# Setup work before a first attention: where an image load, the scan constants and the weight tables stand in a four-layer kernel

## The chip, the cores and the metric

The kernel runs on one core of a Trainium2 chip. The metric is the device time of one execution in microseconds (us). Everything is single precision (f32).

## What is computed

A batch of four images of 128 channels and 64 x 64 pixels (4096 positions) goes through four residual layers. Each layer first group-normalises its input (32 groups of 4 channels).

```python
x = x + attention(gn(x), Wq, bq, Wk, bk, Wv, bv)      # 4096 x 4096 scores per image
x = x + conv5x5(gn(x), kernel_from(weightsxx, weightsidentity, XhatXhat, identity, inds...))
x = x + mamba(gn(x))     # Wx, 4-tap conv, silu, softplus, scan over 4096 steps; forward and reverse half
x = x + conv3x3(gn(x), main_w) + main_b
```

The 5x5 kernel is not given. It is built from two small radial tables: for each of 25 taps the table entry of the tap's radius, times a direction table, plus an identity part. The scan layer keeps 64 states for each of 2 x 64 channels: `h[t] = exp(delta[t]*A) * h[t-1] + delta[t]*x[t]*B[t]`, and `y[t] = sum over states of h[t]*C[t] + D*x[t]`.

## The kernel before

**Setup (L97 to L209).** The ScalarE queue loads the small inputs: `vec`, `wv`, `wm` (the transposed Wq, Wk, Wv, Wx), `wback`, `m3` (the 3x3 weights), `ssm`, `every` (the rates Alog, spread over partitions) and `bv`. From these the kernel makes `wqk` and `bqk` (needed by attention), and the constants of the scan layer: `a_neg`, `sel`, `skip` (L137 to L164), and `wtap`, `edge`, `cbias`, `hbias` (L190 to L209). `wtap` is Wx times each of the four convolution taps; each takes a small matmul (`ptap`, L195) and a VectorE multiply (L198). The pool `early`, which holds `wm`, is closed at L207, and only then are the pools `big` (whole images) and `bg` opened (L1040), so the image tile `x` lies on memory that `early` had.

**Stages.** `images()` (L1025) is one long Python generator of "work": for image 0 the attention, the 5x5 convolution and the preparation of the scan's operands, then the same for images 1, 2 and 3, then the ends and the 3x3 convolutions of images 0 to 2. Each step yields an estimated TensorE cost in us (PRODUCT 0.86 for a full matmul, SLOT 0.7, HOP 1.7). `scan_core` (L751) is the other generator: the scan of all four images as 1024 ticks, 256 an image. A tick is one product `db` on GpSimd (L808, 128 x 1024), two exponentials on ScalarE (L801), two scans on VectorE (L818), a product with C on VectorE (L821) or GpSimd (L839), and on every second tick four matmuls `y` on TensorE (L853). The main loop (L1088) takes half a tick and then as much work as a credit allows: PACE 2.9 cost units a tick, 1.5 for the last image. Instructions are put out in the order in which these generators are asked; each engine executes its own queue in that order.

**Attention of image 0 (L361)** runs before any scan. For each of 8 blocks of 512 queries it goes through 32 units; unit u does `scores(u)` (matmul L405, then exp to `pt` on ScalarE, L411), and `values(u-2)` (matmul L417). `pt` lies in a ring of 8 slots (NRING). In this first attention the softmax sums are collected by `side_sums` (L451): even units on VectorE (`sided`), odd units on GpSimd (`sidep`). The exponential of unit u+8 writes the slot of unit u, so it has to wait for the side sum of unit u. `queries` (L372) of the next block comes at unit 17 of each block.

**The 5x5 weights** are built by `build_conv_weights` (L214), a generator with 13 steps: 5 + 6 table rows (a tiny compare L238, a product L242/L244 and a sum L245 of 128 x 1600 each on VectorE), two steps for the identity and direction tables (L254, L255), and a last sum (L257). In `program` (L1062) one step of it is taken for every one unit of the attention, from the first unit on.

**Operands of the scan (L610).** For each image, eight pieces of 512 positions run through a hand-written plan of slots: piece i starts at slot 5i; its last step is at slot 5i + 13. The logarithms that finish softplus need another activation table than the exponentials, so they are batched: `logs` (L707) handles four pieces at a time (HM = 4), at slots 30 and 50. After `logs` come `join` and the store of delta, `drives` (GpSimd, L690) and the store of delta*x. The scan reads its operands back from DRAM, spread over partitions, in chunks c of 1024 positions (two pieces). It is let in by `before(b)` (L1073), once the first four pieces are through, at slot 35. A scan of 256 ticks goes through chunk 0 in its first 64 ticks, and so on.

Of the kernel before, what the change touches and what calls it, by code (L numbers as in the profile page):

```python
# [32 lines left out]
P = 128  # L33
GROUPS = 32
GN_EPS = 1e-5
CH = 1024
MM = 512
# [8 lines left out]
PRODUCT, HOP, SLOT, PACE, ENDPACE, AHEAD = 0.86, 1.7, 0.7, 2.9, 1.5, 4  # L46
# [6 lines left out]
def conv_preact_kernel(  # L53
# [16 lines left out]
    nc = tc.nc  # L70
# [4 lines left out]
    KC = 4  # L75
# [17 lines left out]
    def bank(tag, name):  # L93
        return pools.get(tag, ps).tile([P, MM], F32, tag=tag, name=name)
# [3 lines left out]
    nc.scalar.dma_start(vec, vecs)  # L98
    wv = const.tile([P, C], F32, name="wv")
    nc.scalar.dma_start(wv, mats[:, 2, :])  # L100
    setup = ExitStack()
    early = setup.enter_context(tc.tile_pool(name="early", bufs=1))
    wm = early.tile([P, 4, C], F32, name="wm")
# [21 lines left out]
    def col(i):  # L125
        return vec[:, i : i + 1]
# [10 lines left out]

    NK, NQ = P // SG, NST // NI
    a_neg = const.tile([P, NK * NQ], F32, name="a_neg")
    with tc.tile_pool(name="rates", bufs=1) as tmp:  # L140
        every = tmp.tile([P, NK, NQ, NI], F32, name="every")
        for k in range(NK):
            rates = vecs[k * SG : (k + 1) * SG, ALOG : ALOG + NST].unsqueeze(1)
            nc.scalar.dma_start(
                every[:, k].rearrange("p q j -> p (q j)"),
                rates.to_broadcast([SG, NI, NST]),
            )
        mine = tmp.tile([P, NI], F32, name="mine")
        nc.vector.tensor_reduce(
            mine, ident.rearrange("p (s i) -> p i s", i=NI), AX.X, ALU.add  # L150
        )
        every = every.rearrange("p k q i -> p (k q) i")
        mine = mine.unsqueeze(1).to_broadcast([P, NK * NQ, NI])
# [6 lines left out]
    nc.vector.tensor_reduce(  # L160
        sel, ident.rearrange("p (s i) -> p s i", i=NI), AX.X, ALU.add
    )
    skip = const.tile([P, P], F32, name="skip")
    nc.vector.tensor_scalar(skip, ident, col(DSKIP), None, ALU.mult)  # L164


    wqk = const.tile([P, C], F32, name="wqk")
# [22 lines left out]
    wtap = const.tile([P, KC, C], F32, name="wtap")  # L190
    edge = const.tile([P, KC - 1], F32, name="edge")
    cbias = small.tile([P, 1], F32, tag="cbias", bufs=1, name="cbias")
    for k in range(KC):
        ptap = bank("saz"[k % 3], f"ptap{k}")[:, :C]
        nc.tensor.matmul(  # L195
            ptap, col(CONVW + k).to_broadcast([P, P]), ident, start=True, stop=True
        )
        nc.vector.tensor_tensor(wtap[:, k, :], wm[:, 3, :], ptap, ALU.mult)  # L198
    for t in range(KC - 1):

        nc.vector.tensor_reduce(
            edge[:, t : t + 1], vec[:, CONVW : CONVW + KC - 1 - t], AX.X, ALU.add
        )
    nc.vector.tensor_tensor(cbias, edge[:, 0:1], col(CONVW + KC - 1), ALU.add)
    nc.vector.scalar_tensor_tensor(cbias, cbias, col(BX), col(CONVB), ALU.mult, ALU.add)
    nc.vector.tensor_scalar(edge, edge, col(BX), -1.0, ALU.mult, ALU.mult)
    setup.close()  # L207
    hbias = const.tile([P, 1], F32, name="hbias")
    nc.vector.tensor_scalar(hbias, cbias, 0.5, None, ALU.mult)  # L209


    cw = const.tile([P, NTAP, C], F32, name="cw")
# [397 lines left out]
    def scan_operands(b, xn, mats4, piece):  # L610
# [1 line left out]

        bc, dd, dxd, xcd, xsd = mats4
        pad = KC - 1
        HM = NM // 2

        xc = large(b, f"xc_{b}")[:, :L]
        delta = pools["big"].tile([P, L], F32, tag="xt", name=f"delta_{b}")
# [94 lines left out]
        def at(slot, f, *args):  # L713
            slots.setdefault(slot, []).append((f, args))

        EVERY = 5
        for i in range(NM):
# [22 lines left out]
        at(2, ready.add, (b, "read"))  # L740
# [10 lines left out]
    def scan_core(mats4, ynds, before, widen, result):  # L751
# [18 lines left out]
        def load(i):  # L770
            b, c, d, q, g = ticks[i]
            (bmat, cmat), dd, dxd, xcd, _ = mats4[b]
            if q == 0:
                for name, src in (("de", dd), ("dx", dxd)):
                    t = pools["rep"].tile([P, CH], F32, tag=name, name=f"{name}_{b}_{c}_{d}_{g}")
                    k = d * KG + g
                    src = src[c, k * SG : (k + 1) * SG].unsqueeze(1)
                    nc.sync.dma_start(t, src.to_broadcast([SG, NI, CH]))
                    rep[name, b, c, d, g] = t
            if g == 0:  # L780
                for name, src in (("b", bmat), ("c", cmat)):
                    t = pools["rows"].tile([P, CH], F32, tag=name, name=f"{name}r_{b}_{c}_{d}_{q}")
                    n = d * NST + q * NI
                    nc.sync.dma_start(t, src[c, n : n + NI].unsqueeze(0).to_broadcast([SG, NI, CH]))
                    rows[name, b, c, d, q] = t
            if d == 0 and q == NQ - 2 and g == 0:
                xcs[b, c] = pools["rows"].tile([P, CH], F32, tag="xc", bufs=1, name=f"xcr_{b}_{c}")
                nc.sync.dma_start(xcs[b, c], xcd[c])
# [134 lines left out]
    def program(safe):  # L923
# [113 lines left out]
            ready.add((B - 1, "staged"))  # L1037

        with ExitStack() as es, tc.manual_schedule():
            pools["big"] = es.enter_context(tc.tile_pool(name=f"big{safe}", bufs=1))  # L1040
            pools["bg"] = es.enter_context(tc.tile_pool(name=f"bg{safe}", bufs=2))
# [28 lines left out]
            pools["hc"] = es.enter_context(tc.tile_pool(name=f"hc{safe}", bufs=6))  # L1070
# [2 lines left out]
            def before(b):  # L1073

                nonlocal pace
                while (b, NM // 2) not in ready:
                    next(work)
                if b + 1 == B:
                    pace = ENDPACE
# [21 lines left out]
                pass  # L1101

    program(False)


    fit = small.tile([P, B * NJT], F32, tag="fit", bufs=1, name="fit")
# [71 lines left out]
```

## Time and profile before

| | |
|---|---|
| Time, median of 3 runs | 4684.2 us (4680.76 to 4685.26) |
| Span of the profiled run | 4679.2 us |
| First attention matmul of image 0 (L405) | 40.8 us |
| 5x5 convolution of image 0 (L571) | 542.4 to about 717.5 us |
| First scan instruction (L818) | 789.2 us |
| First attention matmul of image 1 | 812.1 us |
| Last `y` of the scan ends, then the end and 3x3 convolution of image 3 | 4597.6 us, until 4672.6 us |

The profile gives the busy time of each engine (PE is TensorE, PEld its weight loads, DVE VectorE, ACT ScalarE, POOL GpSimd, SP the queue of the synchronous engine), the span cut in 40 slices, groups of instructions by source line, waits with what ended them, and instructions in order of time. In a row of the timeline the first number is the start, the second the duration in us; what stands in square brackets at the end is the idle time before it, and what ended it.

### The profile page before, as it was taken

The page shows a single profiled execution, that of the slowest core. Times are in us where ns is not written, and L with a number is a line of the kernel's source. Part 1 is how long each engine was busy: PE and PEld are TensorE (multiplying, and loading weights), DVE is VectorE, ACT ScalarE, POOL GpSimd, SP SyncE. Part 2 cuts the span into 40 slices and gives each one's busy share as a digit, 9 for nine tenths or more (in the row PEclk, how much of TensorE's full clock was granted, in tenths as well). Part 3 has the DMA queues.
Part 4 walks back from the last instruction along what each step waited for, and adds up shares of the span by engine and source line. Part 5 has one row for each costly group of instructions (what it writes and reads, how often), then busy time and mean ns, then how long its engine had stood idle before and what let it go on. Part 6 is the DMA issues. An engine that isn't in the chain of part 4 may idle for free. (4 is left out here: it accounts for less than half of the span.)

```text
span 4679.2 us, 43928 instructions
## 1 busy us (share of the span) xinstructions
PE 4151.4 (89%) x13840; PEld 1538.3 (33%) x13840; DVE 3764.6 (80%) x3673; ACT 2313.3 (49%) x4166; POOL 3522.0 (75%) x1644
## 2 busy tenths in 40 slices
PE   6999997999999988999999979999999748576767
PEld 3444443333333323333333323333333202121212
DVE  7222104999999998999999999899989899999993
ACT  2333205666665356666654466666543644444431
POOL 2333202898888978898989869888889689999992
PEclk9999998999999999999999989999999968787878
DMA  1000005544444555445444564454445565656561
GB/s 65 0 0 1 0 5 184 186 168 163 163 169 150 178 203 214 155 164 175 169 158 164 187 227 169 157 177 164 168 147 177 201 224 199 229 193 229 186 230 46
DMA packets 210434, 718.90 MB, mean 154 GB/s; under 512 B 24848, under 2 KB 25744, under 8 KB 210064
## 3 DMA queue, kind: packets, MB, share of 16 engines
q1 hardware_dynamic: 208448, 714.69, 43.7%
q8 instruction: 111, 1.82, 0.2%
q10 hardware_dynamic: 1744, 1.32, 0.1%
q14 instruction: 131, 1.07, 0.1%
HBM read 649.07 MB, written 66.85 MB: 153 GB/s over the span
## 5 line engine op out<-in xcount | busy, mean ns | idle before, releaser
L808 POOL TENSOR_TENSOR db<-dx,br 128x1024 f32<-128x1024 f32 x1024 | 2404.4, 2367 | 377.8 <-DVE hc L818 94.8
L801 ACT ACTIVATE da<-de,a_neg 128x512 f32<-128x512 f32 (+1 forms) x1795 | 1343.9, 752 | 926.9 <-DVE da L818 600.3
L405 PE MATMUL sc<-r,x 128*128 128x512 f32 x2048 | 1087.5, 613 | 44.0 <-ACT last L834 16.4
L417 PE MATMUL acc<-pt,v 128*128 128x512 f32 x2048 | 1049.1, 594 | 1.5
L839 POOL TENSOR_TENSOR hc<-hc,cr 128x1024 f32<-128x1024 f32 x392 | 928.5, 2369 | 19.0 <-ACT last L834 15.5
L411 ACT ACTIVATE pt<-sc 128x512 f32<-128x512 f32 x1024 | 604.0, 590 | 613.4 <-PE sc L405 577.8
L821 DVE TENSOR_TENSOR hc<-da,cr 128x512 f32<-128x512 f32 (+1 forms) x1095 | 847.1, 774 | 71.7 <-DVE da L818 0.9
L853 PE MATMUL y<-hc,sel 128*32 128x512 f32 x4096 | 654.0, 653 | 272.7 <-POOL hc L839 247.5
L818 DVE TENSOR_TENSOR_SCAN da<-da,last,db 128x512 f32<-128x512 f32 (+1 forms) x474 | 740.5, 1562 | 16.2 <-POOL db L808 8.9
L571 PE MATMUL pce<-xpe,cw 128*128 128x512 f32 x1600 | 724.6, 606 | 24.8 <-ACT xpe L311 17.8
L818 DVE TENSOR_TENSOR_SCAN da<-da,da,db 128x512 f32<-128x512 f32 x463 | 595.8, 1287 | 26.2 <-ACT da L801 25.8
L405 PEld LDWEIGHTS sc<-r,x 128*128 128x128 f32 x2048 | 358.9, 190 | 642.7 <-issue 385.9
L417 PEld LDWEIGHTS acc<-pt,v 128*128 128x128 f32 x2048 | 388.4, 190 | 498.9 <-issue 480.0
L571 PEld LDWEIGHTS pce<-xpe,cw 128*128 128x128 f32 x1600 | 297.3, 190 | 452.4 <-issue 424.0
L818 DVE TENSOR_TENSOR_SCAN hc<-da,last,db 128x512 f32<-128x512 f32 (+1 forms) x294 | 442.7, 1506 | 2.9 <-POOL db L808 1.2
L818 DVE TENSOR_TENSOR_SCAN hc<-da,hc,db 128x512 f32<-128x512 f32 x308 | 395.1, 1283 | 45.1 <-ACT da L801 15.6
L459 POOL TENSOR_TENSOR sidep<-sidep,pt 128x512 f32<-128x512 f32 x120 | 161.3, 1344 | 307.0 <-ACT pt L411 307.0
L853 PEld LDWEIGHTS y<-hc,sel 128*32 128x32 f32 x4096 | 93.5, 111 | 728.7 <-POOL hc L839 333.2
L571 PE MATMUL pcm<-xpm,m 128*128 128x512 f32 x576 | 287.5, 647 | 31.4 <-ACT xpm L311 31.4
L459 DVE TENSOR_TENSOR sided<-sided,pt 128x512 f32<-128x512 f32 x120 | 90.3, 753 | 249.7 <-ACT pt L411 248.4
L818 DVE TENSOR_TENSOR_SCAN da<-da,db 128x512 f32<-128x512 f32 (+1 forms) x158 | 235.7, 1492 | 17.0 <-ACT da L801 9.3
L834 ACT COPY last<-da 128x1 f32<-128x1 f32 x473 | 74.0, 156 | 270.1 <-DVE hc L821 268.2
(167 smaller groups left out, 2251.9 us busy)
## 6 DMA issues: line engine op xcount, KB each, us to landing
br<-bm SPq DMA_DIRECT2D x512, 512.0 KB, 5.0
cr<-cm SPq DMA_DIRECT2D x512, 512.0 KB, 3.9
de<-dd SPq DMA_DIRECT2D x64, 512.0 KB, 4.6
dx<-dxd SPq DMA_DIRECT2D x64, 512.0 KB, 6.2
x<-in_x_dram SPq DMA_DIRECT2D x16, 512.0 KB, 5.7
xs<-in_x_dram SPq DMA_DIRECT2D x16, 512.0 KB, 6.8
xsd<-xs SPq DMA_DIRECT2D x16, 512.0 KB, 5.1
xcd<-xc SPq DMA_DIRECT2D x16, 512.0 KB, 2.7
```

The lines of the kernel that those rows point to most:

```text
L405: nc.tensor.matmul(sc, xn[:, bass.ts(j, P)], rq[blk], start=True, stop=True)
L411: nc.scalar.activation(pt, sc, AF.Exp)
L417: nc.tensor.matmul(acc[blk], v[:, j, :], ring[:, u % NRING, :], start=j == 0, stop=j == NJT - 1)
L459: eng.tensor_tensor(s, s, ring[:, u % NRING, :], ALU.add)
L571: nc.tensor.matmul(acc.rearrange("p (r w) -> p r w", w=W), weights[:, t, :], xp[:, y : y + RPM, dx : dx + W], start=t == 0, stop=t == k * ...
L801: nc.scalar.activation(da, rep["de", b, c, d, g][:, bass.ts(h, size)], AF.Exp, scale=a_neg[:, at(i)])
L808: nc.gpsimd.tensor_tensor(dbs[i], rep["dx", b, c, d, g], rows["b", b, c, d, q], ALU.mult)
L818: nc.vector.tensor_tensor_scan(h, da, db[:, cut], before, ALU.mult, ALU.add)
L821: nc.vector.tensor_tensor(hc[:, cut], h, rows["c", b, c, d, q][:, cut], ALU.mult)
L834: nc.scalar.copy(last[b][:, at(i)], end)
L839: nc.gpsimd.tensor_tensor(hcs[i], hcs[i], rows["c", b, c, d, q], ALU.mult)
L853: nc.tensor.matmul(y[r : r + SG, :], sel, hcs[i - KG + 1 + gg][:, bass.ts(h, MM)], start=q == 0, stop=False, tile_position=(0, r), skip_gr ...
```

## The change

Three parts. First, the pools `big` and `bg` are opened ahead of `early`, so that the tiles of the first image have memory of their own and their loads depend on nothing in the setup. Second, the constants of the scan leave the setup: they become a generator `scan_constants` of 8 steps, and the loop that ran `build_conv_weights` now runs both, one after the other, taking a step for every four units of the attention in place of one. Third, the operands of image 0's scan are let through in three groups, pieces 0-1, 2-5 and 6-7, and the scan enters when chunk 0 (a quarter) is there. For the other images the groups stay four and four.

```diff
+    lower = ExitStack()
+    pools["big"] = lower.enter_context(tc.tile_pool(name="big", bufs=1))
+    pools["bg"] = lower.enter_context(tc.tile_pool(name="bg", bufs=2))
     setup = ExitStack()
     early = setup.enter_context(tc.tile_pool(name="early", bufs=1))
...
-    with tc.tile_pool(name="rates", bufs=1) as tmp:
-        every = tmp.tile([P, NK, NQ, NI], F32, name="every")
...
-        nc.vector.tensor_tensor(every, every, mine, ALU.mult)
-        nc.vector.tensor_reduce(a_neg, every, AX.X, ALU.add)
-    nc.scalar.activation(a_neg, a_neg, AF.Exp)
-    nc.vector.tensor_scalar(a_neg, a_neg, -1.0, None, ALU.mult)
...
-    for k in range(KC):
-        ptap = bank("saz"[k % 3], f"ptap{k}")[:, :C]
...
-    setup.close()
...
+    def scan_constants():
+        for k in range(KC):
+            ptap = bank("z", f"ptap{k}")[:, :C]
+            nc.tensor.matmul(
+                ptap, col(CONVW + k).to_broadcast([P, P]), ident, start=True, stop=True
+            )
+            yield HOP
+            nc.vector.tensor_tensor(wtap[:, k, :], wm[:, 3, :], ptap, ALU.mult)
+        for t in range(KC - 1):
+            nc.vector.tensor_reduce(
+                edge[:, t : t + 1], vec[:, CONVW : CONVW + KC - 1 - t], AX.X, ALU.add
+            )
...
+        yield HOP
+        mine = early.tile([P, NI], F32, name="mine")
...
+        nc.vector.tensor_tensor(rates, rates, mine, ALU.mult)
+        nc.vector.tensor_reduce(a_neg, rates, AX.X, ALU.add)
+        yield HOP
+        nc.scalar.activation(a_neg, a_neg, AF.Exp)
...
+        nc.vector.tensor_scalar(skip, ident, col(DSKIP), None, ALU.mult)
+        yield HOP
+        nc.vector.tensor_scalar(a_neg, a_neg, -1.0, None, ALU.mult)
+        yield HOP
...
-        def logs(i):
-            for n in range(i, i + HM):
+        def logs(i, j):
+            for n in range(i, j):
                 nc.scalar.activation(us[n], us[n], AF.Ln)
...
-        for i in (0, HM):
-            t = EVERY * (i + HM - 1) + 15
-            at(t, logs, i)
-            for n, c in enumerate(range(i * MM // CH, (i + HM) * MM // CH)):
+        PER = CH // MM
+        cuts = (0, PER, NM - PER, NM) if b == 0 else (0, NM // 2, NM)
+        for i, j in zip(cuts, cuts[1:]):
+            t = EVERY * (j - 1) + 15
+            at(t, logs, i, j)
+            for n, c in enumerate(range(i // PER, j // PER)):
                 at(t + 1 + n, join, c)
                 at(t + 3 + n, drives, c)
-            at(t + 3 + HM * MM // CH, ready.add, (b, i + HM))
+                at(t + 4 + n, ready.add, (b, "operands", c))
...
                     with tc.tile_pool(name="tables", bufs=1) as tmp:
-                        for _ in build_conv_weights(tmp):
-                            next(work)
+                        for _ in chain(scan_constants(), build_conv_weights(tmp)):
+                            for _ in range(4):
+                                next(work)
                     while (0, "attended") not in ready:
                         next(work)
                 del pools["fill"]
+                setup.close()
...
             def before(b):
                 nonlocal pace
-                while (b, NM // 2) not in ready:
+                while (b, "operands", 0) not in ready:
                     next(work)
```

More of the change, by code (lines that the diff above doesn't have):

```diff
@@ L139, in conv_preact_kernel @@
     a_neg = const.tile([P, NK * NQ], F32, name="a_neg")
-    with tc.tile_pool(name="rates", bufs=1) as tmp:
-        every = tmp.tile([P, NK, NQ, NI], F32, name="every")
[L142 to L150, printed above, removed]
-        )
-        every = every.rearrange("p k q i -> p (k q) i")
-        mine = mine.unsqueeze(1).to_broadcast([P, NK * NQ, NI])
-        nc.vector.tensor_tensor(every, every, mine, ALU.mult)
-        nc.vector.tensor_reduce(a_neg, every, AX.X, ALU.add)
-    nc.scalar.activation(a_neg, a_neg, AF.Exp)
-    nc.vector.tensor_scalar(a_neg, a_neg, -1.0, None, ALU.mult)
+    every = early.tile([P, NK, NQ, NI], F32, name="every")
+    for k in range(NK):
+        rates = vecs[k * SG : (k + 1) * SG, ALOG : ALOG + NST].unsqueeze(1)
+        nc.scalar.dma_start(
+            every[:, k].rearrange("p q j -> p (q j)"),
+            rates.to_broadcast([SG, NI, NST]),
+        )
     sel = const.tile([P, SG], F32, name="sel")
-    nc.vector.tensor_reduce(
-        sel, ident.rearrange("p (s i) -> p s i", i=NI), AX.X, ALU.add
-    )
     skip = const.tile([P, P], F32, name="skip")
-    nc.vector.tensor_scalar(skip, ident, col(DSKIP), None, ALU.mult)
     wqk = const.tile([P, C], F32, name="wqk")
@@ L192, in conv_preact_kernel @@
     cbias = small.tile([P, 1], F32, tag="cbias", bufs=1, name="cbias")
-    for k in range(KC):
-        ptap = bank("saz"[k % 3], f"ptap{k}")[:, :C]
-        nc.tensor.matmul(
-            ptap, col(CONVW + k).to_broadcast([P, P]), ident, start=True, stop=True
-        )
-        nc.vector.tensor_tensor(wtap[:, k, :], wm[:, 3, :], ptap, ALU.mult)
-    for t in range(KC - 1):
+    hbias = const.tile([P, 1], F32, name="hbias")
+    def scan_constants():
[10 more added lines that the diff above has]
+            )
+        nc.vector.tensor_tensor(cbias, edge[:, 0:1], col(CONVW + KC - 1), ALU.add)
+        nc.vector.scalar_tensor_tensor(cbias, cbias, col(BX), col(CONVB), ALU.mult, ALU.add)
+        nc.vector.tensor_scalar(edge, edge, col(BX), -1.0, ALU.mult, ALU.mult)
+        nc.vector.tensor_scalar(hbias, cbias, 0.5, None, ALU.mult)
+        yield HOP
+        mine = early.tile([P, NI], F32, name="mine")
+        nc.vector.tensor_reduce(
+            mine, ident.rearrange("p (s i) -> p i s", i=NI), AX.X, ALU.add
+        )
+        rates = every.rearrange("p k q i -> p (k q) i")
+        mine = mine.unsqueeze(1).to_broadcast([P, NK * NQ, NI])
+        nc.vector.tensor_tensor(rates, rates, mine, ALU.mult)
+        nc.vector.tensor_reduce(a_neg, rates, AX.X, ALU.add)
+        yield HOP
+        nc.scalar.activation(a_neg, a_neg, AF.Exp)
@@ L201, in conv_preact_kernel @@
         nc.vector.tensor_reduce(
-            edge[:, t : t + 1], vec[:, CONVW : CONVW + KC - 1 - t], AX.X, ALU.add
+            sel, ident.rearrange("p (s i) -> p s i", i=NI), AX.X, ALU.add
         )
-    nc.vector.tensor_tensor(cbias, edge[:, 0:1], col(CONVW + KC - 1), ALU.add)
-    nc.vector.scalar_tensor_tensor(cbias, cbias, col(BX), col(CONVB), ALU.mult, ALU.add)
-    nc.vector.tensor_scalar(edge, edge, col(BX), -1.0, ALU.mult, ALU.mult)
-    setup.close()
-    hbias = const.tile([P, 1], F32, name="hbias")
@@ L209, in conv_preact_kernel @@
-    nc.vector.tensor_scalar(hbias, cbias, 0.5, None, ALU.mult)
+        nc.vector.tensor_scalar(skip, ident, col(DSKIP), None, ALU.mult)
+        yield HOP
+        nc.vector.tensor_scalar(a_neg, a_neg, -1.0, None, ALU.mult)
+        yield HOP
     cw = const.tile([P, NTAP, C], F32, name="cw")
@@ L614, in scan_operands @@
         pad = KC - 1
-        HM = NM // 2
         xc = large(b, f"xc_{b}")[:, :L]
@@ L773, in load @@
             if q == 0:
+                assert (b, "operands", c) in ready
                 for name, src in (("de", dd), ("dx", dxd)):
@@ L1039, in program @@
         with ExitStack() as es, tc.manual_schedule():
-            pools["big"] = es.enter_context(tc.tile_pool(name=f"big{safe}", bufs=1))
-            pools["bg"] = es.enter_context(tc.tile_pool(name=f"bg{safe}", bufs=2))
+            if safe:
+                pools["big"] = es.enter_context(tc.tile_pool(name="big_safe", bufs=1))
+                pools["bg"] = es.enter_context(tc.tile_pool(name="bg_safe", bufs=2))
             banks = ExitStack()
@@ L1103, in conv_preact_kernel @@
     program(False)
+    lower.close()
     fit = small.tile([P, B * NJT], F32, tag="fit", bufs=1, name="fit")
```

## The prediction

> **What bounds the kernel now.** I read the page's busy times and slices first, then the timeline of the first 110 us, the waits of the queue that issues loads, and the stages around the first scan. From the page:
>
> ```profile
> PE 4151.4 (89%) x13840; PEld 1538.3 (33%) x13840; DVE 3764.6 (80%) x3673; ACT 2313.3 (49%) x4166; POOL 3522.0 (75%) x1644
> PE   6999997999999988999999979999999748576767
> DVE  7222104999999998999999999899989899999993
> ```
>
> A slice is 117 us. TensorE is full from slice 2 to about 31, VectorE in the last eight. So up to about 3700 us whatever leaves TensorE idle in a stage that nothing else overlaps is paid once, at full size: all later work stands behind it. The holes are in slice 1, at slice 7 and at the image changes. The change touches the first two.
>
> The start, from the timeline and from the waits of the load queue in the first 30 us:
>
> ```profile
> 14.81 0.29 DVE L198 TENSOR_TENSOR wtap<-wm,ptap 128x128 f32<-128x128 f32 x1 [0.88 <-PE ptap L195]
> 15.17 1.81 SPq L929 DMA_DIRECT2D x<-in_x_dram  x4
> 24.50 0.37 DVE L281 BATCH_NORM_AGGREGATE gcols<-st_a 128x2 f32<-128x48 f32 x1
> 27.99 2.37 ACT L311 ACTIVATE x<-x,nb_a,rs_a 128x1024 f32<-128x1024 f32 x2 [17.25 <-POOL nb_a L306]
> 40.77 2.94 PE L405 MATMUL sc<-r,x 128*128 128x512 f32 x6 [0.78 <-ACT r L374]
> ```
>
> ```profile
> SPq L929 <- DVE wtap L198: 5.5, 1, 5.5
> ```
>
> The image load is issued at 15.17, right after the last `wtap` product: `x` lies on the memory of `wm`. Attention starts at 40.77 as the end of one chain: load, statistics, normalise, keys, queries.
>
> The first attention, from the timeline:
>
> ```profile
> 71.43 1.82 DVE L245 TENSOR_TENSOR picked<-picked,cw 128x1600 f32<-128x1600 f32 x1
> 73.18 0.68 DVE L459 TENSOR_TENSOR sided<-sided,pt 128x512 f32<-128x512 f32 x1
> 73.95 1.09 ACT L411 ACTIVATE pt<-sc 128x512 f32<-128x512 f32 x2 [8.08 <-DVE hitid L238]
> 74.60 2.08 PE L405 MATMUL sc<-r,x 128*128 128x512 f32 x2 [5.47 <-ACT pt L411]
> 83.77 1.13 PE L372 MATMUL pr<-x,wqk 128*128 128x512 f32 x2 [3.44 <-ACT pt L411]
> 148.39 1.02 PE L372 MATMUL pr<-x,wqk 128*128 128x512 f32 x2
> 207.99 1.02 PE L372 MATMUL pr<-x,wqk 128*128 128x512 f32 x2
> ```
>
> VectorE, packed with table work, reaches the side sum `sided` late; the exponential that wants the ring slot waits 8 us for it; TensorE waits for that. The `pr` rows are the clock of this stage: one a block, 59.60 us apart undisturbed (148.39 to 207.99).
>
> The entry of the first scan, by stages (columns: length, then PE, PEld, DVE, ACT, POOL busy, TensorE clock, DMA share, GB/s):
>
> ```profile
> 718.00:757.00 39.00, 31.72 (x110) 10.92 (x112) 10.62 (x24) 21.54 (x34) 0.74 (x2) 0.91 0.46 162
> 757.00:778.00 21.00, 18.37 (x65) 5.75 (x61) 16.57 (x31) 16.95 (x28) 5.80 (x4) 1.00 0.47 188
> 778.00:812.00 34.00, 20.05 (x76) 12.77 (x74) 21.04 (x21) 26.87 (x45) 20.30 (x9) 0.71 0.72 257
> 812.00:850.00 38.00, 37.95 (x128) 13.64 (x129) 32.14 (x32) 22.97 (x49) 33.46 (x15) 0.95 0.59 222
> ```
>
> ScalarE is the busiest from 757 to 812 after TensorE's stretched matmuls (79 to 81%); from 812 TensorE is full again. So the scan is not the bound there, nor later while attention runs beside it (900 to 1000 us: PE 99%, DVE 92%, POOL 89%).
>
> **What the Trainium skill says.** "DMA: Bandwidth & Descriptors", Issuing engines are not separate DMA queues: loads of several queues share 16 engines and interleave, so the early image load will share with the setup loads. The trace has 340 to 418 GB/s from 17 to 24 us, with two queued loads; nothing yet shows image and setup together. "SBUF — State Buffer", SBUF: two separate sides: a VectorE instruction with two SBUF inputs and a GpSimd one lock each other out whole. The trace agrees: `sidep` takes 2.01 us on average from 40 to 110 and 1.26 later; L245 takes 2.30 there although L244 of its size takes 1.83. "TensorE: Matmul & The Clock Gate", Part 1: an idle TensorE falls to half clock and has to warm up again. The trace agrees: a pair of matmuls takes 2.08 us at 74.60 and 1.02 undisturbed, at a mean clock of 0.87 from 60 to 100. "ScalarE: Activation LUTs", What ACT_TABLE_LOAD costs: 1283 ns for the load and 1380 ns of drain. The trace shows 1.28 for the load; I take that.
>
> **The change part by part.**
>
> *Image load at once.* Setup now issues `x` at about 0.75 instead of 15.17. A floor for its landing: `x` is 2.1 MB, and the loads that go with it (`vec`, `wv`, `wm`, `wback`, part of `m3`) 0.5 to 1.1 MB; 2.6 to 3.2 MB at 380 GB/s is 7 to 8.5 us, plus some 2 us until data flow (issue 15.17, rate up at 17): landing at 9.5 to 11. In before the last piece landed at about 23.2 (issue 16.6 + 6.6) and the aggregate came at 24.50, 1.3 later. So the aggregate comes at 11 to 12.5, plus 0.3 for `wqk` and `bqk` ahead of it in the queue: gain 11.7 to 13.2, less up to 1.5 if ScalarE, whose queue still issues `m3`, `every` and `bv` behind those landings and must load its table (1.28), is late. I take 12.3; ends 10 and 13.3. The setup constants that leave cost nothing more: they were what the load waited for.
>
> *Tables and constants spread.* Loss in before, from the `pr` clock: unit 17 should come 34 matmuls x 0.858 = 29.2 us after 40.77, that is at 70.0; it came at 83.77, 13.8 late. From there to the next `pr` 64.6 instead of 59.6: 5.0 more. Together 18.8. Now one step per four units, 4 x 1.716 = 6.9 us. The costliest step on VectorE: 0.17 + 1.83 + 2.3 + two side sums of 0.9 = 6.1. It fits, and the longest stretch ahead of a side sum is 4.3 us, against some six units (10 us) of slack in the ring. 21 steps end at unit 84 of 256, long before the convolution needs `cw`. Added on the path: four `ptap` matmuls, 0.6 us each as in setup (L195 there: eight instructions in 1.63 + 0.79), and three of them wait for the product before them on VectorE, up to 0.3: some 3. The settling of blocks 0 and 1 (2.5 us of VectorE) falls among table steps, and its matmul may wait a few tenths. Other constants are below 0.5 us each and hidden by TensorE. Net gain 15.5; ends 11 and 18.5.
>
> *Early entry.* Slots run 1.31 us apart (6.55 for five, 743.28 to 749.83). Entry moves from slot 35 to 24: some 14 us, or three to four ticks of about 3.7 us. But one batch of logarithms more means two more table loads, 2.6 us, and three ticks add 3 x 1.5 = 4.5 us of ScalarE, the busiest engine there; I let attention of image 1 start 3 us later against the end of the convolution. From there to the end of image 1's convolution TensorE is the bound and the pace in ticks is fixed, so the lead of three ticks is not cashed in that stretch. It is cashed at the change of images, where VectorE and ScalarE are 90% and 79% busy and TensorE 79% (1700 to 1800): about half of 3.3 ticks x 3.7, 6 us. What waits for what: a `y` matmul put out early in TensorE's queue would hold the keys of image 1 behind it; in the changed order the first stands after the fifth group of keys, about where 803 us was, and its ticks would be done by about 790. Net 3; ends -5 and 12. The same readiness for images 1 to 3 comes one slot earlier, which is nothing while the pace rules.
>
> Sum: 12.3 + 15.5 + 3 = 30.8, and 4684.2 - 30.8 = 4653. Nothing after 812 us changes in kind, so it should arrive whole.
>
> **Rivals.** (1) Spreading relieves only half: locks between VectorE and GpSimd and the waits of `ptap` leave 9 of 18.8, so 12.3 + 8 + 2 = 22: 4662. For it: DVE at 6.1 of 6.9 is tight; against: the ring's slack. (2) The scan's lead counts in full, because VectorE at 92% is nearly the bound: 12.8 + 17 + 12 = 42: 4642. Against: TensorE at 99% beside it. (3) Slower: each of 21 steps leaves one 1.83 pass uncovered (38 us in place of 18.8, a loss of 19), and the entry makes image 1 start 8 us late, against 12 from the load: 15 slower, 4699. For it: in-order queues with new waits in all of them; against: slack as computed.
>
> **How the numbers follow.** Main 0.6; rival 1 0.17; rival 2 0.19; rival 3 0.04. Ends summed: 10 + 11 - 5 = 16 and 13.3 + 18.5 + 12 = 44, so 4640 to 4668; I take 4638 to 4668, which leaves out rival 3 and some spread of the others. Faster 0.95, same 0.01, slower 0.04.
>
> **What would show it.** First L405 near 28.5 instead of 40.8. First `pr` of a next block some 31 us after it instead of 43, the following one 59.6 to 61 later, and no 8 us waits of `pt`. End of image 0's convolution near 690 (717.5 - 27.8). First scan instruction about 56 us after that end, instead of 72, and image 1's attention 97 after it instead of 94. Image 2's attention (1789 to 1792 before) some 30 earlier. It would be wrong if the last image landed after 13 us, if `pt` still waited for `sided`, or if the ticks' lead opened holes on TensorE.

## The result, and the profile after

| | before | changed |
|---|---|---|
| Time, median | 4684.05 us (4680.76 to 4685.26) | 4664.63 us (4663.02 to 4668.27, 4 runs) |
| Ratio to before, 95% interval | | 0.9961 (0.9943 to 0.9978) |
| Span of the profiled run | 4679.2 us | 4661.2 us |

The change saves 19.4 us (0.4%). The forecast was 4653 with a range of 4638 to 4668: the direction and the range hold (the range by 3 us), and 11.4 of the 30.8 forecast us are missing. A second timing of the same kernel beside other runs gave 4664.90 against 4687.61 (0.9950, 0.9936 to 0.9963), a saving of 22.7.

The page of the changed kernel, busy times and slices:

```profile
PE 4156.2 (89%) x13840; PEld 1542.3 (33%) x13840; DVE 3766.5 (81%) x3678; ACT 2317.4 (50%) x4171; POOL 3522.5 (76%) x1644
PE   8999998999999988999999979999999858576767
DVE  4622106989999988999999989898999999999993
```

The work is the same. The first slice of TensorE rose from 6 to 8, and VectorE's table work is spread over two slices (7 and 2 became 4 and 6): the hole at the start did get smaller. TensorE's seventh slice rose from 7 to 8 too, but only because the stage in it comes earlier; the hole at the first scan got longer, as will be seen. The rest is read from times of single events.

The start of the changed kernel, from its timeline (start, duration, engine, line, operation; in brackets the idle time before it and what ended it):

```profile
0.74 5.97 SPq L942 DMA_DIRECT2D x<-in_x_dram  x4
11.84 1.29 DVE L330 BATCH_NORM_STATS2 st_a<-x 128x6 f32<-128x512 f32 x2 [4.40 <-DMA x<-in_x_dram]
15.05 0.37 DVE L291 BATCH_NORM_AGGREGATE gcols<-st_a 128x2 f32<-128x48 f32 x1
18.53 2.37 ACT L321 ACTIVATE x<-x,nb_a,rs_a 128x1024 f32<-128x1024 f32 x2 [4.13 <-POOL nb_a L316]
30.63 0.38 PE L188 MATMUL ptap<-ident,vec 128*128 128x128 f32 x2
31.57 1.98 PE L415 MATMUL sc<-r,x 128*128 128x512 f32 x4 [0.56 <-ACT r L384]
61.62 0.59 PE L382 MATMUL pr<-x,wqk 128*128 128x512 f32 x1
119.55 2.77 DVE L255 TENSOR_TENSOR picked<-picked,cw 128x1600 f32<-128x1600 f32 x1
121.23 1.02 PE L382 MATMUL pr<-x,wqk 128*128 128x512 f32 x2
```

Two things are to be seen. The image is issued at 0.74, but the four issues take until 6.71 (in before they took 1.81), and the aggregate comes at 15.05. And the `pr` clock is clean: 30.05 us from the first attention matmul to the first `pr` (43.0 in before), then 59.61 to the next. The waits of the changed kernel, first those of the load queue in the first 8 us, then ScalarE's for `pt` from 28 to 110 us (engine and line, what it waited for: us in total, times, longest):

```profile
SPq L942 <- DMA vec<-in_vecs_dram: 3.2, 1, 3.2
SPq L942 <- DMA wv<-in_mats_dram: 1.2, 1, 1.2
...
ACT pt L421 <- PE sc L415: 49.3, 43, 3.0
```

The load queue waited for the landing of two small inputs before it issued the later quarters of the image, and by the trace the last quarter landed only at 13.56. The exponentials now wait for scores, which is their input; there is no row any more in this window in which `pt` waits for a side sum on VectorE.

The entry of the first scan by stages (length, then PE, PEld, DVE, ACT, POOL busy, TensorE clock, DMA share, GB/s):

```profile
690.00:750.00 60.00, 50.59 (x173) 16.58 (x171) 25.05 (x52) 37.95 (x60) 7.56 (x7) 0.94 0.60 211
750.00:800.00 50.00, 30.83 (x116) 16.27 (x115) 38.17 (x40) 39.34 (x67) 36.64 (x16) 0.76 0.72 255
800.00:850.00 50.00, 49.22 (x182) 17.81 (x181) 44.00 (x45) 31.17 (x64) 44.96 (x21) 1.00 0.39 144
```

From 750 to 800 TensorE is at 62%, with ScalarE at 79% and GpSimd and VectorE at 73 to 76%: scan work stands there now while image 1's attention has not begun. From 800 TensorE is full again, as in before from 812.

Seen over the whole kernel, the gain runs like this (us earlier than in before, from the timelines; a tick is named by its `db` product):

| | end of the 5x5 conv of image 0 | attention of image 1 (`pr`) | of image 2 | of image 3 | tick 752 | end of the span |
|---|---|---|---|---|---|---|
| changed | 26.6 | 21.1 | 22.7 | 17.3 | 22.1 | 18.0 |

26.6 us were won by the end of the convolution; 5.5 of them are lost again at once, in the entry of the scan, and nothing is added later. The last columns are less sure than the first: each is one profiled execution, and executions of one kernel drift apart by some us towards the end.

### The profile page after: what moved, and what is told of

Same layout as the page of the kernel before. It is cut to its first block, busy times and chain, and to the rows that moved or that the text cites. A ratio compares the mean times of both kernels' runs of the same rounds, so it can differ in the third digit from the quotient of the medians.

```text
span 4661.2 us, 43922 instructions
## 1 busy us (share of the span) xinstructions
PE 4156.2 (89%) x13840; PEld 1542.3 (33%) x13840; DVE 3766.5 (81%) x3678; ACT 2317.4 (50%) x4171; POOL 3522.5 (76%) x1644
## 5 line engine op out<-in xcount | busy, mean ns | idle before, releaser
L415 PE MATMUL sc<-r,x 128*128 128x512 f32 x2048 | 1085.1, 612 | 30.2 <-ACT last L847 15.6
L581 PE MATMUL pce<-xpe,cw 128*128 128x512 f32 x1600 | 724.1, 605 | 27.2 <-ACT xpe L321 20.2
L831 DVE TENSOR_TENSOR_SCAN da<-da,da,db 128x512 f32<-128x512 f32 x465 | 598.5, 1287 | 26.9 <-ACT da L814 26.6
L831 DVE TENSOR_TENSOR_SCAN hc<-da,hc,db 128x512 f32<-128x512 f32 x309 | 396.4, 1283 | 46.2 <-ACT da L814 16.4
L449 PE MATMUL zp<-pt,ones 128*32 128x512 f32 x1536 | 208.4, 603 | 0.0
```

Of the source, the lines that this page charges most:

```text
L415: nc.tensor.matmul(sc, xn[:, bass.ts(j, P)], rq[blk], start=True, stop=True)
L449: nc.tensor.matmul(zp[blk][g * 32 : (g + 1) * 32, :], ones[:, :32], ring[:, (u - 3 + g) % NRING, :], start=j == 3, stop=j == NJT - 1, tile ...
L581: nc.tensor.matmul(acc.rearrange("p (r w) -> p r w", w=W), weights[:, t, :], xp[:, y : y + RPM, dx : dx + W], start=t == 0, stop=t == k * ...
L831: nc.vector.tensor_tensor_scan(h, da, db[:, cut], before, ALU.mult, ALU.add)
```

## The experiments

All kernels are variants of the changed or the old kernel. Each is compared with runs of before on its own chip.

**Which part brings what: each part alone on the old kernel.**

The load alone: the pools `big` and `bg` are opened ahead of `early`, and the constants stay in the setup.

```diff
+    lower = ExitStack()
+    pools["big"] = lower.enter_context(tc.tile_pool(name="big", bufs=1))
+    pools["bg"] = lower.enter_context(tc.tile_pool(name="bg", bufs=2))
     setup = ExitStack()
```

> The kernel before with the first part alone: image memory opened ahead of the setup's, constants and tables where they were. If the parts add: first attention matmul about 31.5 us instead of 40.8 and 9 us less, 4675. Rival 'setup constants hold the chain': the products of the constants stand among the statistics on VectorE and TensorE, the matmul comes 2 to 4 us later than 31.5, and the gain is 5 to 7 us: 4678.

Measured: 4678.68 (4673.56 to 4685.45) against 4686.56, 0.9983 (0.9976 to 0.9990), 7.9 us faster. Its timeline shows that the constants left in the setup now stand in the way, because the image no longer waits for something slower than they are:

```profile
18.12 1.63 PE L198 MATMUL ptap<-ident,vec 128*128 128x128 f32 x6
20.95 0.29 DVE L201 TENSOR_TENSOR wtap<-wm,ptap 128x128 f32<-128x128 f32 x1 [0.35 <-PE ptap L198]
22.40 2.37 ACT L314 ACTIVATE x<-x,nb_a,rs_a 128x1024 f32<-128x1024 f32 x2 [5.52 <-POOL nb_a L309]
34.37 1.12 PE L408 MATMUL sc<-r,x 128*128 128x512 f32 x2 [0.78 <-ACT r L377]
```

The `wtap` products are mixed among the steps of the group normalisation on VectorE; normalising starts 6.45 us after the aggregate (15.95 to 22.40), and in the changed kernel 3.48 (15.05 to 18.53). The first attention matmul stands at 34.37 instead of 31.57; 0.9 of these 2.8 us is the later aggregate, so moving the constants out is worth some 2 to 3 us at the start.

The spread of the tables alone:

```diff
                         for _ in build_conv_weights(tmp):
-                            next(work)
+                            for _ in range(4):
+                                next(work)
```

> The kernel before with the tables taken one step per four units of the attention, nothing else (the constants of the scan stay in the setup). By the row clock of the changed kernel the spreading is worth 17.9 us in the first attention: first matmul at 40.8 as before, next row of pr 30 us after it, end of image 0's convolution near 699.5. If stages add, 18 us less than before. Rival 'later stages give some back': 10 to 14.

Measured: 4670.83 (4664.21 to 4675.36) against 4685.80, 0.9968 (0.9956 to 0.9980), 15.0 us faster. The first attention matmul is at 41.40, and the timeline has the clock of the blocks:

```profile
70.78 1.02 PE L372 MATMUL pr<-x,wqk 128*128 128x512 f32 x2
...
130.38 1.02 PE L372 MATMUL pr<-x,wqk 128*128 128x512 f32 x2
```

The first `pr` came at 83.77 in before and the second at 148.39, so the second is 18.0 us earlier here; the convolution ends 16.9 earlier, and the ticks from 0 to 264 start 16.4 to 19.0 earlier. This loss was simply taken out, and it arrives nearly whole at the end.

The early entry alone: the third part of the change on the old kernel, with load and tables as they were.

```diff
+        cuts = (0, PER, NM - PER, NM) if b == 0 else (0, NM // 2, NM)
...
-                while (b, NM // 2) not in ready:
+                while (b, "operands", 0) not in ready:
```

> The kernel before with the third part alone: operands of image 0 in groups 0-1, 2-5, 6-7, entry at slot 24. Theory 'the third part costs by itself': image 1's attention 97 to 98 us after the convolution instead of 91.7, a lead of some 18 us at the first tick, 5 to 8 by tick 16, none at tick 264, and a time 5 to 9 us above before. Rival 'it only costs beside the other two parts': within 2 us of before, or faster.

Measured: 4690.49 (4687.62 to 4695.31) against 4685.80, 1.0011 (1.0003 to 1.0019): 4.7 us slower (1.4 to 8.9). The three parts alone give -7.9 - 15.0 + 4.7 = -18.2, and the whole gave -19.4 and -22.7, so they add up within the scatter (none of the three takes the constants out of the setup, which is worth the 2 to 3 us above); the third part is a loss.

Where it loses is seen from the end of image 0's convolution to the first `pr` of image 1. In before (stage row, then the waits of TensorE in that stage):

```profile
717.50:809.20 91.70, 68.07 (x245) 28.93 (x245) 47.46 (x74) 64.67 (x102) 24.04 (x14) 0.87 0.55 201
```

```profile
PE pv L338 <- ACT v L343: 9.8, 5, 5.5
...
PE pb L660 <- ACT bs L665: 4.1, 3, 1.6
```

With the early entry alone:

```profile
718.30:815.50 97.20, 68.70 (x252) 29.00 (x252) 57.95 (x84) 71.18 (x113) 37.49 (x20) 0.87 0.63 224
```

```profile
PE pb L659 <- ACT last L835: 7.1, 1, 7.1
...
PE pv L338 <- ACT v L343: 5.8, 4, 2.0
...
PE pv L338 <- ACT last L835: 3.8, 1, 3.8
```

TensorE has practically the same work (68.07 and 68.70), ScalarE 6.5 us more of it in the stage, and the stage is 5.5 us longer. Two new holes of 7.1 and 3.8 us stand on TensorE, and each ends when ScalarE has come to a certain place in its queue (`last`, L835, is a small copy of the scan and only the last thing done there): TensorE waits for copies that ScalarE delivers after the logarithms and the ticks put ahead of them. The waits for `v` and `bs` shrank by 6.6 us in exchange (9.8 to 5.8, and 4.1 to 1.5; the row of the 1.5 is not shown), so some 4 of the 5.5 us are waits of this kind. The benefit would have to come from the ticks' lead, and that one goes like this (start of a tick's `db` against before, minus is earlier):

| | tick 0 | 16 | 240 | 252 | 264 | attention of image 1 |
|---|---|---|---|---|---|---|
| entry alone | -17.2 | -5.9 | -5.8 | -8.7 | +6.4 | +6.4 |
| changed | -44.8 | -33.2 | -33.2 | -36.2 | -20.2 | -21.1 |
| load alone | -7.6 | -7.3 | -7.4 | -7.3 | -7.0 | -7.3 |
| spread alone | -17.0 | -16.7 | -17.2 | -16.9 | -16.9 | -16.7 |

Two thirds of the 17 us lead of the entry are gone by tick 16; the rest is carried through image 0's scan and is gone at tick 264, the ninth of image 1. There the ticks of these four kernels sit within 0.9 us of the shift that the attention of image 1 had 1000 us earlier. The rows of GpSimd and of the load queue around that change of images, first before, then the entry alone:

```profile
1796.15 4.67 POOL L808 TENSOR_TENSOR db<-dx,br 128x1024 f32<-128x1024 f32 x2
1803.45 2.36 POOL L808 TENSOR_TENSOR db<-dx,br 128x1024 f32<-128x1024 f32 x1 [2.64 <-PE sc L405]
...
1792.32 1.90 SPq L929 DMA_DIRECT2D xs<-in_x_dram  x4
1794.26 0.75 SPq L784 DMA_DIRECT2D br<-bm  x1
```

```profile
1796.80 4.65 POOL L809 TENSOR_TENSOR db<-dx,br 128x1024 f32<-128x1024 f32 x2 [1.44 <-DMA br<-bm]
1809.88 2.34 POOL L809 TENSOR_TENSOR db<-dx,br 128x1024 f32<-128x1024 f32 x1 [8.42 <-DMA br<-bm]
...
1800.54 1.76 SPq L930 DMA_DIRECT2D xs<-in_x_dram  x4
1802.35 0.57 SPq L785 DMA_DIRECT2D br<-bm  x1
...
SPq L930 <- DMA dxd<-xc: 4.7, 1, 4.7
```

With the lead, GpSimd stands still for 8.42 us and waits for a read of image 1's operands (`br`). The read itself stands in the load queue right behind `xs`, the second load of image 2 (2 MB), in both kernels, and with the entry alone that load had waited 4.7 us for the store `dxd` of image 1's operands. So tick 264 is tied to the place where image 2 begins rather than to the first matmuls of image 1: over all 14 traces of this study it starts 14.3 to 17.3 us after image 2's attention, but 989 to 1006 us after image 1's; the four kernels above happen to agree on both. A scan that runs ahead only reaches this wait sooner. The lead is not all lost, though: from image 1's attention to image 2's it takes 977.5 us with the entry alone and 980.0 in before, a gain of 2.5.

**Which feature of the entry costs: grouping or timing.** On the changed kernel, with everything else left in place. Two groups for every image, entry one slot before the old one:

```diff
-        cuts = (0, PER, NM - PER, NM) if b == 0 else (0, NM // 2, NM)
+        cuts = (0, NM // 2, NM)
```

> The changed kernel with its third part undone: operands of image 0 in two groups of four pieces, the scan let in at slot 34 (before: 35). Theory 'entry costs': load and spreading keep their 27 us, image 1's attention starts about 94 us after the end of image 0's convolution as before (101 in the changed kernel), and the time is 7 to 8 us under the changed kernel's 4664.6: about 4657. Rival 'entry is neutral, the 8 us are lost later': same time as the changed kernel within 2 us, because the loss comes at the image changes whatever the entry.

Three groups (pieces 0-1, 2-3 and 4-7), but the scan waits for the second chunk as before, so the extra batch of logarithms stands alone:

```diff
-        cuts = (0, PER, NM - PER, NM) if b == 0 else (0, NM // 2, NM)
+        cuts = (0, PER, NM // 2, NM) if b == 0 else (0, NM // 2, NM)
...
-                while (b, "operands", 0) not in ready:
+                while (b, "operands", 1 if b == 0 else 0) not in ready:
```

> Three groups of logarithms (pieces 0-1, 2-3, 4-7), but the scan still enters at slot 34: the extra pair of table loads alone, without the early entry. Theory 'the early ticks do it': like two groups plus at most the 2.6 us of the two loads, image 1's attention 94 to 97 us after the convolution, time about 4657 to 4660. Rival 'the extra batch does it': 99 to 101 us after the convolution, time about 4663.

The same three groups, and the scan enters with the first chunk (only the first line of the edit above, that of `cuts`):

> Three groups of logarithms (0-1, 2-3, 4-7) and the scan entering at slot 24, as in the changed kernel; only the second batch stands elsewhere (slot 30 instead of 40). Theory 'the early ticks do it': 100 us or more after the convolution and about 4664, like the changed kernel. Rival 'the extra batch, or where it stands, does it': close to the run with three groups and late entry.

Measured on one chip, before 4686.56: two groups 4656.95 (0.9940, 0.9923 to 0.9956), three groups late 4655.51 (0.9932, 0.9915 to 0.9949), three groups early 4659.14 (0.9944, 0.9927 to 0.9961). All three lie closer together than their runs scatter, which fits the rival of the third expectation, and all seemed faster than the changed kernel, which had not run beside them. So it was run on another chip beside two of them, unedited:

> The changed kernel once more, beside the next three on one chip, to tell the difference between its entry and the others' apart from a difference between chips. Theory 'its entry costs': 6 to 8 us above the run with two groups. Rival 'it was the chip, and runs of one kernel spread by 9 us': within 2 us of it.

> Two groups of four pieces, entry at slot 34, again. Theory 'the changed entry costs': 29 to 30 us under the kernel before, 6 to 8 under the changed kernel. Rival: the same as the changed kernel within 2 us.

> Three groups 0-1, 2-3, 4-7 with the early entry, again. Its single profile ended like that of the two groups. Theory 'early entry is neutral in the end, the second batch of logarithms at slot 40 in the changed kernel is what costs': equal to two groups within 2 us, the changed kernel 5 us or more above. Rival 'early entry itself costs': near the changed kernel, at least 4 us above two groups.

Measured, before 4687.61: changed 4664.90 (4663.61 to 4666.66), two groups 4655.99 (4653.27 to 4658.45; 0.9929, 0.9916 to 0.9943), groups 2-2-4 entered early 4657.01 (4655.02 to 4659.97; 0.9933, 0.9919 to 0.9947). No single run of the changed kernel reaches one of the others: its entry costs 8.9 us against two groups and 7.9 against the other grouping. So at a credit of 2.9 a lead bought with groups 2-4-2 loses; where it loses has to be read from the traces.

Three groups late costs nothing in the total, and its stage from the convolution's end to image 1's `pr` is 95.1 us, that of two groups 95.5 and 95.6:

```profile
688.80:783.90 95.10, 66.64 (x245) 28.11 (x244) 51.05 (x77) 68.32 (x107) 28.81 (x15) 0.88 0.56 200
```

So the extra batch and its two table loads are not the price. (The expectations counted to the first matmul of the scores, which stands a little later: by that event it is 94.6 us in before, 98.9 here, 99.0 with two groups and 101.1 in the changed kernel. The 94 to 97 expected for two groups and for three groups late did not come: most of the delay of image 1 is there with the late entry too, one slot earlier than in before, and the runs do not show from what.) In the changed kernel the timeline shows such a batch:

```profile
754.36 1.28 ACT L718 ACT_TABLE_LOAD   x1
755.65 2.19 ACT L718 ACTIVATE u<-u 128x512 f32<-128x512 f32 x4
757.86 1.28 ACT L814 ACT_TABLE_LOAD   x1
759.16 0.69 ACT L814 ACTIVATE da<-de,a_neg 128x512 f32<-128x512 f32 x1
759.79 1.22 ACT L321 ACTIVATE x<-x,nb_a,rs_a 128x1024 f32<-128x1024 f32 x1
760.92 0.56 ACT L674 COPY bs<-pb 128x512 f32<-128x512 f32 x1
761.53 2.07 PE L669 MATMUL pb<-xc,bdiag 128*128 128x512 f32 x2 [7.11 <-ACT last L847]
```

"ScalarE: Activation LUTs" in the Trainium skill, What ACT_TABLE_LOAD costs, gives 1283 ns for the load and 1380 ns of drain. The load is 1.28 here; of the drain this trace shows nothing, since the first `Ln` starts 0.01 us after the load and the load 0.02 after the instruction before (753.67 + 0.67). The place makes a hole: the batch of four pieces, a scan exponential and image 1's normalisation stand ahead of a `bs` copy in ScalarE's queue, and TensorE's next `pb` stands still for 7.11 us. But this hole is not what the 8.9 us are: the same 7.1 us stand in the fastest kernel of the study (credit 2.94, next experiment), and at image 1's attention the changed kernel is only some 2 to 3 us behind two groups.

The length of the entry alone does not settle it either: groups 2-2-4 have the longest entry (98.3 us) and are about as fast as two groups, whose scan starts 8.6 us later against the convolution (68.9 and 60.3 after its end). The loss comes late. From image 1's attention to image 2's the kernels with the early entry (changed and 2-2-4, two traces each) need 971.8 to 979.2 us, and those with the late one (two groups, three groups late, two halves below) 986.3 to 990.6: here the lead is worth 7 us and more. From image 2's attention to the end the first need 2891.8 to 2897.7 us and the second 2881.0 to 2882.4, and what was won is lost again. At credit 2.9 the early entry was neutral at best, and with the grouping 2-4-2 it loses. The traces show where, not why.

**Does the scan's lead fail because of the order of instructions at the change of images?** The credit gives image 0's scan 2.9 cost units a tick. In the changed order, a block of work about three times as large as in before (18 and 6 us by the estimated costs) is put out ahead of tick 248 with no tick between, because image 1's operands have to be ready first. My theory: this forced block makes the scan stand still, and a slightly larger credit, which spreads the block over the ticks of image 0, lets the lead survive. Once on the changed kernel and once on the 2-2-4 grouping:

```diff
                 while (b, "operands", 0) not in ready:
                     next(work)
+                pace = 2.94 if b == 0 else PACE
```

> The changed kernel with the work's credit in image 0 raised from 2.9 to 2.94 a tick, so that image 1's operands come in the order of instructions before the ticks that need them: the block of 18 us of work put out without a tick ahead of tick 248 becomes 6 us as in the kernel before. Theory 'the scan's lead is lost because the scan stands still in that block': tick 264 comes 6 to 10 us earlier than in the changed kernel, the time 4 to 8 us less, about 4658. Rival 'TensorE is the bound up to there, so the ticks only run slower': tick 264 within 2 us of the changed kernel, time the same.

> Groups 0-1, 2-3, 4-7 with the early entry, and credit 2.94 in image 0. Theory 'scan stands still': 3 to 8 us under the same groups at 2.9 (4657), the best so far. Rival: the same as those within 2 us.

Measured, before 4685.80, with the edit on the changed kernel 4643.02 (4641.06 to 4644.02; 0.9907, 0.9891 to 0.9922), on the 2-2-4 grouping 4662.02 (4655.57 to 4663.18; 0.9944, 0.9931 to 0.9958). The first is the fastest kernel of the study, 42.8 us faster than before and 22 below the changed kernel's times, which were taken on other chips; the second is no better than without the edit (0.9944 and 0.9933). The theory falls all the same. The forced block did shrink in both: the most matmuls that TensorE does there between two groups of `y` are 66 in the changed kernel and 68 with 2-2-4, 42 in both variants with 2.94, and 40 in before. But tick 264 came 18.6 and 15.6 us earlier than in before, no gain over the changed kernel (20.2) and over 2-2-4 (29.1). For the changed kernel the rival was right about tick 264, though not about the time. The gain of the first arises elsewhere (each row is from one profiled execution, and those scatter by some us: the load alone, 7.9 faster in the median, had a span 1.8 longer than that of before):

| earlier than before, us | attention of image 1 | image 2 | image 3 | tick 752 | tick 800 | tick 928 | end of span |
|---|---|---|---|---|---|---|---|
| changed | 21.1 | 22.7 | 17.3 | 22.1 | 32.8 | 15.8 | 18.0 |
| changed, credit 2.94 | 22.2 | 19.1 | 26.2 | 25.0 | 38.7 | 35.0 | 37.0 |
| 2-2-4, credit 2.94 | 22.6 | 16.1 | 19.6 | 17.2 | 19.6 | 19.9 | 18.4 |
| 2-2-4 | 23.9 | 32.0 | 25.4 | 29.5 | 39.7 | 22.9 | 24.4 |
| two groups | 23.7 | 17.4 | 18.4 | 22.6 | 28.8 | 19.6 | 25.0 |
| entry alone | -6.4 | -3.9 | -7.2 | -4.0 | 5.7 | -12.2 | -10.7 |

Up to tick 752 the changed kernel and its variant with the larger credit differ by 3 us; the remaining 16 come in the last 270 ticks. Ticks 800 to 928 as stages, in before, the changed kernel, and the changed kernel with credit 2.94:

```profile
3860.20:4271.50 411.30, 296.06 (x888) 85.57 (x888) 399.57 (x233) 186.49 (x293) 396.81 (x179) 0.83 0.60 211
```

```profile
3827.40:4255.70 428.30, 298.72 (x886) 87.58 (x886) 408.72 (x248) 189.66 (x297) 398.04 (x183) 0.81 0.59 203
```

```profile
3821.50:4236.50 415.00, 299.88 (x896) 86.13 (x896) 400.67 (x233) 186.23 (x294) 396.92 (x178) 0.82 0.61 213
```

VectorE is the busiest here in all three (97%, 95%, 97%), with GpSimd close behind (96%, 93%, 96%). The changed kernel has 15 more VectorE instructions in this stretch, 9.1 us more of busy time, and 19.6 us of idle time against 11.7. So a part of its lead at tick 800 is a loan: ticks ran ahead of other work of VectorE, which then is done between the later ticks. With credit 2.94 that work was done before, and the lead stays. That these 15 instructions come late is shown; but two groups has 12 more than before here too, and 2-2-4 has 14, so they do not tell the changed kernel from those. Why the order falls out as it does, and so why 2.94 helps one grouping and not the other, is not shown. It stays open, and 2.94 is a value found rather than a rule. Two groups with 2.94 was not run, so whether the fastest kernel owes anything to the early entry is open too.

**Why the load brought 9.2 and not 12.3.** On the two-group kernel the image comes as two loads of 1 MB instead of four of 512 KB, so that fewer issues can be held up:

```diff
-            yield from load(xn, b)
+            if b == 0:
+                for h in range(2):
+                    nc.sync.dma_start(xn[:, bass.ts(h, L // 2)], xf[b][:, bass.ts(h, L // 2)])
+                    yield 0.0
+            else:
+                yield from load(xn, b)
```

> Two groups, and image 0 loaded as two halves of 1 MB in place of four quarters. In the changed kernel the third and fourth quarter were issued only at 4.85 and 6.4 us, after vec and wv had landed[...]. Theory 'the late issues cost': both halves are issued by 1.7 us, the aggregate of the statistics comes near 12.3 instead of 15.05, the first attention matmul near 28.5, and the time is 2 to 3 us under the run with two groups. Rival 'the engines are full anyway': same landing, first matmul at 30 to 31.5, no gain.

Measured: 4655.82 (4652.95 to 4659.13), against 4655.99 for two groups beside it: no difference. Its timeline:

```profile
0.74 0.86 SPq L954 DMA_DIRECT2D x<-in_x_dram  x2
10.72 1.27 DVE L330 BATCH_NORM_STATS2 st_a<-x 128x6 f32<-128x512 f32 x2
13.55 0.37 DVE L291 BATCH_NORM_AGGREGATE gcols<-st_a 128x2 f32<-128x48 f32 x1
30.18 1.13 PE L415 MATMUL sc<-r,x 128*128 128x512 f32 x2 [0.56 <-ACT r L384]
```

Both halves are issued by 1.60, and by the trace the second has landed at 8.89, where the last quarter landed at 13.56 in the changed kernel. So the late issues are what made the image late: issued at once it lands even before the 9.5 to 11 of the forecast. Yet the aggregate comes only 1.5 us earlier than in the changed kernel. The waits of this kernel in the first 17 us say why:

```profile
PE pw L164 <- DMA wm<-in_mats_dram: 9.8, 1, 9.8
...
DVE st_a L330 <- DMA x<-in_x_dram: 6.2, 1, 6.2
...
DVE wt L165 <- PE pw L164: 1.6, 1, 1.6
```

VectorE waits for the image once, for its first half. Then the copy `wt`, which leads to `wqk`, stands in its queue ahead of the later statistics and waits for a product of `wm`, a weight that now lands after the image. So the next step of the chain binds: 1.6 us of waiting, and the statistics that stand behind it, take back most of what the landing won. How much is left cannot be read from single executions: the nine traces of kernels with the four quarters and the constants moved out have the last landing at 11.3 to 13.9 us, the aggregate at 13.05 to 15.53 and the first attention matmul at 28.38 to 32.21, and the halves, with 13.55 and 30.18, lie inside. The total shows no gain, as the rival had it.

## Why the prediction was right, and where it was short

The main case, faster with the gain of three parts, holds for two of them; the third has the wrong sign. So the direction was right for the right reason, but 4653 was missed by 11.6 us, and the range holds only because it was wide on the side of small gains: the result is 3 us inside its end. Of the three signs of being wrong that the prediction named, two came: the last quarter landed after 13 us (13.56), and the ticks' lead opened holes on TensorE (7.1 and 3.8 us).

- **What bounds the kernel.** Holds: a loss that leaves TensorE idle at the start is paid in full. The spread alone was worth 16.9 us at the convolution's end and 15.0 in the total.
- **Image load at once: 12.3 expected, 9.2 measured** (40.77 to 31.57), just outside the ends of 10 and 13.3. This is one execution: over the nine traces above the gain on 40.77 is 8.6 to 12.4. The mechanism holds, the landing was mis-sized: last landing at 13.56 instead of 9.5 to 11, aggregate at 15.05 instead of 11 to 12.5. The step assumed that nothing holds up the issues; the trace has 3.2 and 1.2 us of waits in the load queue for other loads, and without them (two halves) the image lands at 8.89. It also put the weights' product at 0.3 us; with the halves it is what the statistics wait for.
- **Tables and constants spread: 15.5 expected, 17.9 measured** (second `pr` 107.62 after the first attention matmul in before, 89.66 now), within the ends. The term of 3 for the `ptap` matmuls was too high: their pair takes 0.38 us in a busy TensorE, and the first `pr` is only 0.9 us later than undisturbed (30.05 against 29.2). "SBUF — State Buffer" in the Trainium skill, SBUF: two separate sides, on the lock between VectorE and GpSimd, agrees with this trace too: the sum on L255 (L245 in before) takes 2.77 us at 119.55, more than the 2.3 I costed, and the GpSimd sum beside it at 118.28 takes 2.35 instead of 1.26. It is hidden all the same, as the step said: from 28 to 240 us no wait of `pt` for the tables or side sums is longer than 1.2 us.
- **The two together: 27.8 expected at the second `pr`, 27.2 measured** (148.39 to 121.23), and 26.6 at the convolution's end, near 690 as forecast (690.9). The errors of the two cancel.
- **Early entry: +3 expected, a loss of 4.7 alone (1.4 to 8.9).** This is the step that failed, in both its terms, though -4.7 still lies within its ends of -5 and 12. First, image 1's attention was let start 3 us later against the convolution's end; it starts 5.5 later by `pr` (97.2 against 91.7), and 6.5 later by the first matmul of the scores, which the forecast counted (101.1 where it had 97, and 94.6 in before). Second, the lead "is cashed at the change of images, 6 us": alone on the old kernel it brings 2.5 there. Busy shares of 90% on VectorE at the change made me think that the scan was the bound. In fact the tick at the change waits for a read that stands in the load queue behind the load of image 2. Against the kernels with late entry the change of images does bring 7 us and more, and the rest of the kernel takes them back. The price was also argued in part from the wrong item: table loads, which by the three-groups-late run cost nothing.
- **"Nothing after 812 us changes in kind, so it should arrive whole."** Not so: between image 2's attention and the end the changed kernel drifts from 22.7 to 17.3, to 22.1 and to 18.0 us, and a credit changed by 1.4% moved some 20 us with one grouping. The order in which work and ticks interleave is itself worth some 10 to 20 us in this kernel, and none of my ends had that. What in the order does it stays open.
- **The rivals.** The measured time is nearest to rival 1 (4662), but not for its reason: spreading relieved everything, not half. Rival 2 (the lead counts in full) falls with the time and with the tick table. Rival 3 has the sign of the third part right and its own reason wrong: no table pass stood uncovered, and the 8 us at image 1 were 5.5 (6.5 by the scores).

In the sum: 30.8 expected; 0.6 less from the first two parts (27.2 for 27.8); the third -4.7 alone for +3, which is 7.7 less; together 22.5, beside 19.4 and 22.7 measured in two comparisons.

## What to carry to other kernels

Give the first load memory that no setup work uses, take setup work out of the chain that follows it, and spread it at a rate that its engine can hold per unit of the work it hides in: 15 and 8 us came from that, and each could be forecast to about 3 us from the chain of loads and the distance of a recurring matmul (their sum came nearer, because the errors cancelled). Then look at what stands next in the chain: with the image in time, a weight product was what it waited for. Before letting a stage start earlier, ask what it waits for at its far end, the place of its reads in the load queue included: a lead is then only waiting moved, while its instructions in the in-order queues delay other work. After any such move, try neighbouring credits on the chip: the best kernel here, 4643.0 us, is the changed one with 2.94 in place of 2.9 for the first image.

## What was not expected of the hardware

An early load can be held back by loads that it has nothing to do with: the third and fourth quarter of the image waited for the landing of `vec` and `wv`, 3.2 and 1.2 us, although they share no memory, and two larger loads in place of four did not wait and had the whole image in at 8.89 us instead of 13.56. Why the queue waits so, the runs do not show. And moving the first scan 17 us earlier left nothing of its lead at the ninth tick of the next image, although VectorE was 91% busy just before it (54.53 of 60 us from 1700 to 1760 in before): the tick's read stood behind a 2 MB load in the queue.
